# Two cross-attention layers on one core: layer 1's rows left unscaled before q, and a new order of the first batch's projections

## The chip, the cores and the metric

The kernel runs on one core of a Trainium2 chip. The core has a tensor engine (PE, with its weight loads shown apart as PEld), a vector engine (DVE), a scalar engine (ACT), a GpSimd engine (POOL) and a sync engine (SP), which here does nothing but issue DMAs. Each engine works through its own queue in order, and engines wait for one another on semaphores. The metric is the device time of one execution in microseconds (us); lower is better. All data is float32.

## The reference

The input x has the shape (4, 1024, 512) and a context of (4, 1024, 384) goes with it. Two cross-attention layers follow each other. Cut to what matters:

```
# layer 0: 16 heads of 64
h    = layernorm(x) * gamma + beta
Q, K, V = h @ Wq, ctx @ Wk, ctx @ Wv
attn = softmax(Q K^T) * 64**-0.5
x    = x + (attn V) @ Wo + bo

# layer 1: 16 heads of 32
xn   = x * rsqrt(mean(x*x) + 1e-5) * norm_w      # per row of x
q    = rotate((xn @ wq) by heads, cos, sin)
k, v = rotate((ctx @ wk) by heads, cos, sin), ctx @ wv
q    = q / max(norm(q), 1e-12)                   # per row and head
k    = k / max(norm(k), 1e-12)
out  = x + softmax(q k^T * sqrt(32)) v @ wout
```

In layer 1, q is brought to unit length per head. A factor that a whole row of x carries into q therefore drops out of q again, except in the comparison with 1e-12.

## The kernel before

**Batches.** The four batches run one after the other. In each, layer 0 goes through eight pairs of heads (p = 0 to 7) and, in each pair, eight blocks of 128 queries (`Attention0.step`). A step puts scores on PE (L366), takes the row maximum on DVE (L391), exponentials on ACT (L392), scales the rows on POOL (L397) and turns 32x32 blocks on DVE (L400); every second step sixteen DMAs on SP (L411, tile eT) finish the transposition, and a product with v (L427, tile av) follows two steps later. Layer 1 works in two halves of eight heads (`Attention1.step`): scores L576, exponentials L586, sums of the exponentials on DVE (L592 adds two tiles of 128x512, L596 two of 128x1024), products L615 and L626, and at the end of a block a reciprocal on DVE (L633).

**Filling work.** All other work for PE (projections, transposes, output products) is cut into units with a cost, kept in a queue (`Units`). Each attention step takes units from the queue until their costs fill the time that the step is given. The order of the units in the queue is written out by hand; units that cost 0.0 put nothing on PE. PE's instructions come out in the order in which units are taken.

**The rows of x.** `norm_units` makes, for each half of the rows of a batch (four tiles of 128 rows), the units "stats", "apply" and "turn". For layer 1, "stats" squares the rows on ACT with their sum as a second output (L222), and on POOL scales the sum and adds eps (L223, tile ve) and raises it to the power -0.5 (L168, tile rs). "apply" multiplies the four tiles by rs on DVE (L235, tile xn). "turn" transposes them on PE in four groups of four 128x128 blocks (L246, tile pth); each group fills one PSUM bank, which ACT copies out with the column factor norm_w (L252, tile hT). For layer 0 the same units do a layer norm (L216, L231, L248).

**The chains of q and k in layer 1.** `rotated_chains` projects two tiles of rows into one PSUM bank (L164, tiles q_p and k_p). `rotate` then squares it on ACT (L477), rotates it on DVE (L479 to L482; L479 to L481 read the bank, and the last of them frees it), sums the squares by heads (L484, tile q_s), and on POOL takes the maximum with 1e-24 (L486, tile q_m, 128x16), the power -0.5 (L168, tile q_r) and the product with the rows (L490, tile rot). Later the rows are transposed on PE (L498, tile q_t) and copied by ACT (L503). There are eight chains of q in a batch, four in each half of the heads. `weave` puts a chain's last part two chains behind its first.

**Between the layers.** The output products of layer 0's last two pairs go first (tile po, added to x by L294). Then come the statistics of the first half of the rows, a chain of k, the second last product of layer 0 (L427), "apply", "turn", and the first chain of q. The second half of the rows gets its statistics, "apply" and "turn" inside layer 1's first steps, between chains.

**PSUM.** `bank` hands out four banks in turn in layer 0 and three in layer 1 (the fourth then holds the attention product). A bank that comes round again can be written when its last reader is done.

**The start.** In the first batch nothing runs beside the loads, so the order is written apart (L676 to L684): "first" is done before the attention, "rest" is taken by its first three steps and must be used up when step 3 begins, "later" follows. The unit "begin" of pair p loads the weights of pair p + 1 (`pair_load`, L306, three DMAs on SP) into one of two buffers.

The functions that the change touches:

Of the kernel before, what the change touches and what calls it, by code (L numbers as in the profile page):

```python
# [28 lines left out]
F32 = mybir.dt.float32  # L32
AF = mybir.ActivationFunctionType
ALU = mybir.AluOpType
AX = mybir.AxisListType

P = 128
S = 1024
NT = S // P
DQ = 512  # L40
NQ = DQ // P
# [9 lines left out]
EPS = 1e-5  # L51
EPS_L2 = 1e-12
# [56 lines left out]
def xattn_kernel(ctx: ExitStack, tc: tile.TileContext, a: dict, out: bass.AP):  # L109
    nc = tc.nc  # L110
# [87 lines left out]
            for h in range(2)  # L198
        ]

    def norm_units(b, layer, hT, rows):

        got = {}

        def stats(h):
            src = got[h] = rows(h) if layer else got[h]
            rs = sb.tile([P, 4], F32, tag="rs", bufs=2, name=f"rs{layer}_{b}_{h}")
            ve = sb.tile([P, 4], F32, tag="ve", bufs=2, name=f"ve{layer}_{b}_{h}")
            mv = None
            if layer == 0:  # L210
                mv = sb.tile([P, 4, 2], F32, tag="mv", bufs=2, name=f"mv_{b}_{h}")
                for t in range(4):
                    st = sb.tile([P, 6], F32, tag="st", bufs=2, name=f"st_{b}_{h}_{t}")
                    nc.vector.bn_stats(st, src[t])
                    nc.vector.bn_aggr(mv[:, t, :], st)
                nc.gpsimd.tensor_scalar(ve, mv[:, :, 1], 1.0, EPS, ALU.mult, ALU.add)  # L216
                xn = src
            else:
                ss = sb.tile([P, 4], F32, tag="ms", bufs=2, name=f"ss_{b}_{h}")
                xn = [sb.tile([P, DQ], F32, tag="row", bufs=4, name=f"xn_{b}_{h}_{t}") for t in range(4)]  # L220
                for t in range(4):
                    nc.scalar.activation(xn[t], src[t], AF.Square, accum_out=ss[:, t : t + 1])  # L222
                nc.gpsimd.tensor_scalar(ve, ss, 1.0 / DQ, EPS, ALU.mult, ALU.add)  # L223
            rsqrt(rs, ve)
            got[h] = src, xn, mv, rs

        def apply(h):
            src, xn, mv, rs = got[h]
            for t in range(4):
                if layer == 0:  # L230
                    nc.vector.tensor_scalar(  # L231
                        xn[t], src[t], mv[:, t, 0:1], rs[:, t : t + 1], ALU.subtract, ALU.mult
                    )
                else:
                    nc.vector.tensor_scalar_mul(xn[t], src[t], rs[:, t : t + 1])  # L235
            got[h] = xn

        def load(h):
            got[h] = rows(h)

        def turn_over(h, k):
            if k == 0:
                hT.append(sb.tile([P, NQ, 512], F32, tag="hT", bufs=2, name=f"hT{layer}_{b}_{h}"))
            pp = bank(f"pth{layer}_{b}_{h}_{k}")
            for t in range(4):
                nc.tensor.transpose(pp[:, t * P : (t + 1) * P], got[h][t][:, k * P : (k + 1) * P], ident)  # L246
            if layer == 0:
                nc.scalar.activation(  # L248
                    hT[h][:, k, :], pp, AF.Identity, bias=cols[:, 1, k : k + 1], scale=cols[:, 0, k : k + 1]
                )  # L250
            else:
                nc.scalar.activation(hT[h][:, k, :], pp, AF.Copy, scale=cols[:, 2, k : k + 1])  # L252

        return [
            {
                "load": [(0.0, lambda h=h: load(h))],
                "stats": [(0.0, lambda h=h: stats(h))],
                "apply": [(0.0, lambda h=h: apply(h))],
                "turn": [(0.45, lambda h=h, k=k: turn_over(h, k)) for k in range(NQ)],
            }  # L260
            for h in range(2)
        ]
# [174 lines left out]
    TH = 2  # L437
# [10 lines left out]
        nc.sync.dma_start(wq, a["wq"][:, f0:f1].rearrange("(n p) m -> p n m", p=P))  # L448
        return wq

    def rotated_chains(dst, src, nk, w, name, tmp):

        hd, nh = HD1 // 2, TH * FH // HD1
        tiles = {}

        def heads(ap):
            return ap.rearrange("p (t h d) -> p t h d", t=TH, d=HD1)

        def spread(ap):
            return ap.unsqueeze(2).to_broadcast([P, TH, FH // HD1, ap.shape[2]])  # L460

        def project(t0, i, k):
            if i == 0 and k == 0:
                tiles[t0] = [bank(f"{name}_p{t0}")]
                if which["from"] == 0:
                    which["kept"] = which["n"]
            pp = tiles[t0][0]
            t = t0 + i
            lhsT = src[t // 4][:, k, (t % 4) * P : (t % 4 + 1) * P]
            matmul(pp[:, i * FH : (i + 1) * FH], lhsT, w(k), k == 0, k == nk - 1)  # L470
            if i == TH - 1 and k == nk - 1:
                rotate(t0, pp)

        def rotate(t0, pp):

            t1, t2, sq = tmp.take()
            nc.scalar.activation(sq, pp, AF.Square)  # L477
            c_, s_ = cos[:, t0 : t0 + TH, :], sin[:, t0 : t0 + TH, :]
            nc.vector.tensor_mul(heads(t1), heads(pp), spread(c_))  # L479
            nc.vector.tensor_mul(heads(t2)[:, :, :, :hd], heads(pp)[:, :, :, hd:], spread(s_[:, :, :hd]))  # L480
            nc.vector.tensor_mul(heads(t2)[:, :, :, hd:], heads(pp)[:, :, :, :hd], spread(s_[:, :, hd:]))  # L481
            nc.vector.tensor_add(t1, t1, t2)  # L482
            ss = sb.tile([P, nh], F32, tag="ss", bufs=2, name=f"{name}_s{t0}")
            nc.vector.tensor_reduce(ss, sq.rearrange("p (h d) -> p h d", d=HD1), AX.X, ALU.add)  # L484
            sm = sb.tile([P, nh], F32, tag="sm", bufs=2, name=f"{name}_m{t0}")
            nc.gpsimd.tensor_scalar_max(sm, ss, EPS_L2 * EPS_L2)  # L486
            ri = sb.tile([P, nh], F32, tag="ri", bufs=2, name=f"{name}_r{t0}")
            rsqrt(ri, sm)
            t1h = t1.rearrange("p (h d) -> p h d", d=HD1)
            nc.gpsimd.tensor_mul(t1h, t1h, ri.unsqueeze(2).to_broadcast([P, nh, HD1]))  # L490
            tiles[t0] = t1

        def turn_over(t0):
            t1 = tiles.pop(t0)
            pt = bank(f"{name}_t{t0}")
            for g in range(2):
                for i in range(TH):
                    nc.tensor.transpose(  # L498
                        pt[:, (g * TH + i) * P : (g * TH + i + 1) * P],
                        t1[:, i * FH + g * P : i * FH + (g + 1) * P],  # L500
                        ident,
                    )
            nc.scalar.copy(dst()[:, :, t0 * P : (t0 + TH) * P], pt.rearrange("p (g t) -> p g t", g=2))  # L503

        return [
            (
                [(0.44, lambda t0=t0, i=i, k=k: project(t0, i, k)) for i in range(TH) for k in range(nk)],
                [],
                [(0.45, lambda t0=t0: turn_over(t0))],
            )  # L510
            for t0 in range(0, NT, TH)
        ]
# [132 lines left out]
    def flat(lists):  # L645
        return [u for lst in lists for u in lst]

    def prepare_units(b):

        st = {"ct": [], "hT": [], "pairs": [{} for _ in range(NPAIR)]}  # L650
        w = {}
# [16 lines left out]
        def order(other):  # L668
# [7 lines left out]
            if b == 0:  # L676
# [2 lines left out]
                first = cts[0]["turn"] + norms[0]["stats"] + pairs[0]["k"][:NC_] + norms[0]["apply"]  # L679
                first += cts[1]["turn"] + pairs[0]["k"][NC_:] + norms[1]["stats"]  # L680
                first += norms[0]["turn"] + pairs[0]["q"][:NQ] + norms[1]["apply"]
                rest = pairs[0]["v"] + norms[1]["turn"] + pairs[0]["q"][NQ:]
                later = flat([pairs[1][c] for c in ("begin", "k", "q", "v")])
                return [(0.0, load)] + flat(loads) + first, rest, later  # L684
            return flat(
                [
# [28 lines left out]
    for b in range(B):  # L715
# [7 lines left out]
        for p in range(NPAIR):  # L723
# [30 lines left out]
            if p == NPAIR - 1:  # L754
# [2 lines left out]
                    xt, lambda n: pairs[n]["vals"], lambda n: wo[3][:, n % 2, :], f"po0_{b}_3", (6, 7)  # L757
                )
                xnT = []
                norms = norm_units(b, 1, xnT, lambda h: xt[4 * h : 4 * h + 4])  # L760
                v = []

                def begin_v():
# [44 lines left out]
        begin("q")  # L808
        kT, qT = kq["k"], kq["q"]
        kT1, qT1 = qk_tile(f"k1_{b}_1"), sb.tile([P, 2, S], F32, tag="raw", bufs=1, name=f"q1_{b}_1")  # L810
        q = rotated_chains(lambda kq=kq: kq["q"], xnT, NQ, lambda k, wq=wq: wq[0][:, k, :], f"q1_{b}_0", tmp)
        k1 = rotated_chains(lambda kT1=kT1: kT1, ct, NC_, lambda k, wk1=wk1: wk1[0][:, k, :], f"k1_{b}_1", tmp)
        q1 = rotated_chains(lambda qT1=qT1: qT1, xnT, NQ, lambda k: wq1[:, k, :], f"q1_{b}_1", tmp)

        work.add(flat(outs[:4]) + norms[0]["stats"] + k1[0][0] + [(AV, att.product)] + norms[0]["apply"])
        work.add(norms[0]["turn"] + q[0][0] + k1[1][0] + k1[0][2] + [(AV, att.product)] + flat(outs[4:]) + q[0][2])
        work.drain()

# [12 lines left out]
        for half in range(2):  # L831
            n = 0
            if half == 0:
                vs = value_chains(att1.v1, wv1, ct, f"pv1_{b}_1")
                first = [q[1], (norms[1]["stats"], [], []), vs[0], (norms[1]["apply"], [], k1[1][2]), k1[2]]
                rest = [(norms[1]["turn"] + q[2][0], [], q[2][2]), k1[3], q[3], q1[0], vs[1], q1[1], q1[2]]
                rest += [q1[3], vs[2], vs[3]]
                chains = first + rest
# [89 lines left out]
```

## Time and profile before

| what | value |
|---|---|
| median of 3 runs | 2922.01 us (2919.55 to 2923.83) |
| the profiled execution | 2913.88 us, its span 2912.1 us |
| PE busy | 2852.3 us (98%) |
| DVE busy | 2186.5 us (75%) |
| ACT busy | 1434.4 us (49%) |
| POOL busy | 935.1 us (32%) |
| L235, the product of rows with rs | 32 instructions on DVE, 13.4 us |
| L168 on rs, both layers | 16 instructions on POOL, 17.1 us |
| L486 on q | 32 instructions on POOL, 18.4 us |
| granted PE clock, mean | 0.999 |

The time of the profiled execution stands beside its span: the span goes from the first to the last instruction in the trace. A line of the trace's answers in order of time gives the start and the duration in us, the engine, the line of the kernel, the operation, the tile written and the tiles read, the shapes, how many instructions were merged, and in brackets how long the engine had stood idle before and for whom it had waited. A line of the waits gives who waited for whom, the sum in us, how often, and the longest. Where a matmul is counted, the trace shows two records for one float32 instruction.

### The profile page before, as it was taken

The page shows a single profiled execution, that of the slowest core. Times are in us where ns is not written, and L with a number is a line of the kernel's source. Part 1 is how long each engine was busy: PE and PEld are TensorE (multiplying, and loading weights), DVE is VectorE, ACT ScalarE, POOL GpSimd, SP SyncE. Part 2 cuts the span into 40 slices and gives each one's busy share as a digit, 9 for nine tenths or more (in the row PEclk, how much of TensorE's full clock was granted, in tenths as well). Part 3 has the DMA queues.
Part 4 walks back from the last instruction along what each step waited for, and adds up shares of the span by engine and source line. Part 5 has one row for each costly group of instructions (what it writes and reads, how often), then busy time and mean ns, then how long its engine had stood idle before and what let it go on. Part 6 is the DMA issues. An engine that isn't in the chain of part 4 may idle for free.

```text
span 2912.1 us, 66608 instructions
## 1 busy us (share of the span) xinstructions
PE 2852.3 (98%) x27336; PEld 1433.1 (49%) x27336; DVE 2186.5 (75%) x2952; ACT 1434.4 (49%) x2265; POOL 935.1 (32%) x776
## 2 busy tenths in 40 slices
PE   8999999999999999999999999999999999999998
PEld 4444455555444444555544445455554445445544
DVE  5677785878777778587777777858777777785877
ACT  4444444666534444466644444446664444444664
POOL 2343353420134335432024433534102343353300
PEclk9999999999999999999999999999999999999999
DMA  5887775010398777401039887730104988772000
GB/s 142 191 185 184 167 171 127 22 36 25 79 198 191 181 173 174 117 22 36 26 88 213 193 184 166 177 91 22 36 25 113 210 192 187 163 174 74 2 2 31
DMA packets 177553, 348.88 MB, mean 120 GB/s; under 512 B 37600, under 2 KB 93152, under 8 KB 177248
## 3 DMA queue, kind: packets, MB, share of 16 engines
q1 hardware_dynamic: 175920, 343.96, 50.1%
q8 instruction: 216, 3.54, 0.5%
q14 instruction: 89, 0.73, 0.1%
q10 hardware_dynamic: 1328, 0.66, 0.1%
HBM read 67.64 MB, written 8.39 MB: 26 GB/s over the span
## 4 chain that ended last, share of the span: by engine, by line
PE 84%; DVE 8%; SPq 3%; DMA 2%; issue 1%; ACT 1%; POOL 1%; DVEq 0%; ACTq 0%
PE s L366 16%; PE av L427 14%; PE po L164 11%; PE s L576 8%; PE pv L164 7%; PE pqT L164 7%; PE av L615 7%; PE pkT L164 5%; PE q_p L164 3%; SPq L411 2%; PE av L626 2%; PE k_p L164 2%; DVE both L592 2%; DMA eT<-e 1%; DVE both L596 1%
## 5 line engine op out<-in xcount | busy, mean ns | idle before, releaser
L391 DVE TENSOR_REDUCE m<-s 128x1 f32<-128x1024 f32 x512 | 603.0, 1219 | 374.9 <-PE s L366 374.4
L586 ACT ACTIVATE e<-s 128x1024 f32<-128x1024 f32 x512 | 496.7, 1022 | 312.4 <-PE s L576 303.9
L397 POOL TENSOR_SCALAR raw<-raw,li 128x1024 f32<-128x1024 f32 x256 | 286.1, 1118 | 724.2 <-DVE li L396 715.7
L366 PE MATMUL s<-qk 64*128 64x512 f32 x2048 | 515.5, 615 | 2.9 <-ACT e L392 2.2
L392 ACT ACTIVATE e<-s,m 128x1024 f32<-128x1024 f32 x256 | 282.9, 1110 | 466.5 <-DVE m L391 217.4
L392 ACT ACTIVATE raw<-s,m 128x1024 f32<-128x1024 f32 x256 | 285.3, 1115 | 454.8 <-DVE m L391 454.8
L427 PE MATMUL av<-eT,v 128*64 128x256 f32 x4096 | 470.1, 382 | 8.2 <-DMA eT<-e 6.9
L397 POOL TENSOR_SCALAR e<-e,li 128x1024 f32<-128x1024 f32 x256 | 286.0, 1118 | 474.3 <-DVE li L396 247.7
L592 DVE TENSOR_TENSOR both<-e 128x512 f32<-128x512 f32 x512 | 341.9, 700 | 114.2 <-ACT e L586 86.9
L427 PEld LDWEIGHTS av<-eT,v 128*64 128x64 f32 x4096 | 286.2, 137 | 227.2 <-issue 88.6
L366 PEld LDWEIGHTS s<-qk 64*128 64x128 f32 x2048 | 183.7, 186 | 281.5 <-issue 165.4
L576 PE MATMUL s<-q,k 32*128 32x256 f32 x4096 | 306.0, 401 | 5.8 <-ACT q L503 2.7
L400 DVE STREAM_TRANSPOSE e<-raw 128x1024 f32<-128x1024 f32 x256 | 309.9, 1228 | 0.4 <-DMA eT<-e 0.4
L400 DVE STREAM_TRANSPOSE e<-e 128x1024 f32<-128x1024 f32 x256 | 310.0, 1229 | 0.2
L576 PEld LDWEIGHTS s<-q,k 32*128 32x128 f32 x4096 | 192.1, 184 | 152.7 <-ACT e L586 71.4
L164 PE MATMUL pqT<-hT,w 128*64 128x512 f32 (+1 forms) x1216 | 240.6, 595 | 2.4 <-ACT hT L248 2.4
L164 PE MATMUL po<-wo,vals 128*64 128x512 f32 x1024 | 234.6, 596 | 0.0
L294 DVE TENSOR_TENSOR x<-x,po 128x512 f32<-128x512 f32 x200 | 131.2, 678 | 89.4 <-PE po L164 88.8
L164 PEld LDWEIGHTS pv<-w,cT 128*64 128x64 f32 (+1 forms) x3360 | 170.4, 132 | 41.6 <-issue 34.8
L164 PE MATMUL pv<-w,cT 128*64 128x128 f32 (+1 forms) x3360 | 184.3, 274 | 0.7 <-ACT hT L248 0.7
L164 PE MATMUL pkT<-cT,w 128*64 128x512 f32 (+1 forms) x912 | 183.7, 598 | 0.0
L596 DVE TENSOR_TENSOR both<-both 128x1024 f32<-128x1024 f32 x128 | 159.7, 1248 | 4.4
(81 smaller groups left out, 2784.6 us busy)
## 6 DMA issues: line engine op xcount, KB each, us to landing
eT<-e SPq DMA_DIRECT2D x2048, 128.0 KB, 2.4
xr<-in_x_dram SPq DMA_DIRECT2D x32, 256.0 KB, 3.8
wo<-in_Wo_dram SPq DMA_DIRECT2D x16, 512.0 KB, 4.7
x<-in_x_dram SPq DMA_DIRECT2D x32, 256.0 KB, 3.8
out_dram<-x SPq DMA_DIRECT2D x32, 256.0 KB, 2.6
w<-in_Wq_dram SPq DMA_DIRECT2D x31, 256.0 KB, 3.1
c<-in_ctx_dram SPq DMA_DIRECT2D x32, 192.0 KB, 3.8
wkv<-in_wkv_dram SPq DMA_DIRECT2D x16, 384.0 KB, 3.3
```

The costliest lines, as they stand in the source:

```text
L164: nc.tensor.matmul(o[rr], lhsT[:, rr], rhs, start=start, stop=stop)
L366: nc.tensor.matmul(sc[j][:, kb * 512 : (kb + 1) * 512], pr["qT"][r[j], i * P : (i + 1) * P], pr["kT"][r[j], kb * 512 : (kb + 1) * 512], st ...
L391: nc.vector.tensor_reduce(m[:, j : j + 1], sc[j], AX.X, ALU.max, negate=True)
L392: nc.scalar.activation(e[j], sc[j].rearrange("p (g s) -> p g s", g=4), AF.Exp, bias=m[:, j : j + 1], accum_out=l[:, j : j + 1])
L397: nc.gpsimd.tensor_scalar(e[j], e[j], li[:, j : j + 1], HD0**-0.5, ALU.mult, ALU.mult)
L400: self.turn = [lambda j=j: nc.vector.transpose(self.e[:, :, i % BQ * 2 + j, :], e[j]) for j in range(2)]
L427: nc.tensor.matmul(av[r[j], :W].rearrange("p (t a i) -> p t a i", t=BQ, a=4), pr["v"][:, k, r[j]], eT[:, j, :, :, k * 32 : (k + 1) * 32], ...
L576: nc.tensor.matmul(sc[j // 2][:, j % 2, c, :], kT[rr, g, k * P : (k + 1) * P], qT[rr, g, qb * WQ : (qb + 1) * WQ], start=True, stop=True,)
L586: nc.scalar.activation(e, sc[u], AF.Exp, scale=float(np.sqrt(np.float32(HD1))))
L592: nc.vector.tensor_add(self.both[:, kk, 2 * u : 2 * u + 2, :], es[u][:, :, 0, :], es[u][:, :, 1, :])
L596: nc.vector.tensor_add(self.both[:, 0], self.both[:, 0], self.both[:, kk])
L615: nc.tensor.matmul(self.av[rr, 0, :], v[g][:, 2 * kk + c, rr], es[j // 2][:, j % 2, c, :], start=first and c == 0, stop=end and c == 1,)
```

## The change

It has two parts. In layer 1 the rows of x are no longer multiplied by rs: "apply" is gone there, the power -0.5 of ve with it, and "turn" transposes x itself. Since q is brought to unit length, the factor matters only in the maximum with 1e-24, which was taken of the scaled q; the sum of squares of the unscaled q is compared with 1e-24 times (mean(x*x) + 1e-5) instead. That bound differs from row to row, so it lies in ve, and the maximum of a chain of q is two instructions of 128x8, one for each tile of rows, with a column of ve as operand, where it was one of 128x16 with a constant. The chains of k keep the constant. ACT's squares go into scratch tiles that nobody reads.

In the first batch the unit "begin" of pair 1 (the loads of pair 2's weights) and the keys of pair 1 go ahead of the second turn of x and the second half of pair 0's q, where they came after both.

```diff
@@ norm_units, stats, layer 1
-                xn = [sb.tile([P, DQ], F32, tag="row", bufs=4, name=f"xn_{b}_{h}_{t}") for t in range(4)]
                 for t in range(4):
-                    nc.scalar.activation(xn[t], src[t], AF.Square, accum_out=ss[:, t : t + 1])
-                nc.gpsimd.tensor_scalar(ve, ss, 1.0 / DQ, EPS, ALU.mult, ALU.add)
+                    square = sb.tile([P, DQ], F32, tag="row", bufs=4, name=f"sq_{b}_{h}_{t}")
+                    nc.scalar.activation(square, src[t], AF.Square, accum_out=ss[:, t : t + 1])
+                e2 = EPS_L2 * EPS_L2
+                nc.gpsimd.tensor_scalar(ve, ss, e2 / DQ, e2 * EPS, ALU.mult, ALU.add)
+                guard.append(ve)
+                return
             rsqrt(rs, ve)
@@ norm_units, apply
-                    nc.vector.tensor_scalar_mul(xn[t], src[t], rs[:, t : t + 1])
@@ rotated_chains, rotate
-            nc.gpsimd.tensor_scalar_max(sm, ss, EPS_L2 * EPS_L2)
+            if guard is None:
+                nc.gpsimd.tensor_scalar_max(sm, ss, EPS_L2 * EPS_L2)
+            else:
+                for t in range(TH):
+                    own = slice(t * nh // TH, (t + 1) * nh // TH)
+                    at = (t0 + t) % 4
+                    nc.gpsimd.tensor_scalar_max(sm[:, own], ss[:, own], guard[(t0 + t) // 4][:, at : at + 1])
@@ prepare_units, order, first batch
-                rest = pairs[0]["v"] + norms[1]["turn"] + pairs[0]["q"][NQ:]
-                later = flat([pairs[1][c] for c in ("begin", "k", "q", "v")])
+                rest = pairs[0]["v"] + pairs[1]["begin"] + pairs[1]["k"] + norms[1]["turn"] + pairs[0]["q"][NQ:]
+                later = pairs[1]["q"] + pairs[1]["v"]
@@ between the layers
-        work.add(flat(outs[:4]) + norms[0]["stats"] + k1[0][0] + [(AV, att.product)] + norms[0]["apply"])
+        work.add(flat(outs[:4]) + norms[0]["stats"] + k1[0][0] + [(AV, att.product)])
@@ layer 1, first half
-                first = [q[1], (norms[1]["stats"], [], []), vs[0], (norms[1]["apply"], [], k1[1][2]), k1[2]]
+                first = [q[1], (norms[1]["stats"], [], []), vs[0], ([], [], k1[1][2]), k1[2]]
```

More of the change, by code (lines that the diff above doesn't have):

```diff
@@ L199, in context_units, with norm_units @@
         ]
-    def norm_units(b, layer, hT, rows):
+    def norm_units(b, layer, hT, rows, guard=None):
         got = {}
@@ L206, in stats @@
             src = got[h] = rows(h) if layer else got[h]
-            rs = sb.tile([P, 4], F32, tag="rs", bufs=2, name=f"rs{layer}_{b}_{h}")
+            if layer == 0:
+                rs = sb.tile([P, 4], F32, tag="rs", bufs=2, name=f"rs{layer}_{b}_{h}")
             ve = sb.tile([P, 4], F32, tag="ve", bufs=2, name=f"ve{layer}_{b}_{h}")
@@ L229, in apply @@
             for t in range(4):
[L230 to L235, printed above, removed]
+                nc.vector.tensor_scalar(
+                    xn[t], src[t], mv[:, t, 0:1], rs[:, t : t + 1], ALU.subtract, ALU.mult
+                )
             got[h] = xn
@@ L449, in half_q_load, with rotated_chains @@
         return wq
-    def rotated_chains(dst, src, nk, w, name, tmp):
+    def rotated_chains(dst, src, nk, w, name, tmp, guard=None):
         hd, nh = HD1 // 2, TH * FH // HD1
@@ L759, in xattn_kernel @@
                 xnT = []
-                norms = norm_units(b, 1, xnT, lambda h: xt[4 * h : 4 * h + 4])
+                guard = []
+                norms = norm_units(b, 1, xnT, lambda h: xt[4 * h : 4 * h + 4], guard)
                 v = []
@@ L810, in xattn_kernel @@
         kT1, qT1 = qk_tile(f"k1_{b}_1"), sb.tile([P, 2, S], F32, tag="raw", bufs=1, name=f"q1_{b}_1")
-        q = rotated_chains(lambda kq=kq: kq["q"], xnT, NQ, lambda k, wq=wq: wq[0][:, k, :], f"q1_{b}_0", tmp)
+        q = rotated_chains(lambda kq=kq: kq["q"], xnT, NQ, lambda k, wq=wq: wq[0][:, k, :], f"q1_{b}_0", tmp, guard)
         k1 = rotated_chains(lambda kT1=kT1: kT1, ct, NC_, lambda k, wk1=wk1: wk1[0][:, k, :], f"k1_{b}_1", tmp)
-        q1 = rotated_chains(lambda qT1=qT1: qT1, xnT, NQ, lambda k: wq1[:, k, :], f"q1_{b}_1", tmp)
-        work.add(flat(outs[:4]) + norms[0]["stats"] + k1[0][0] + [(AV, att.product)] + norms[0]["apply"])
+        q1 = rotated_chains(lambda qT1=qT1: qT1, xnT, NQ, lambda k: wq1[:, k, :], f"q1_{b}_1", tmp, guard)
+        work.add(flat(outs[:4]) + norms[0]["stats"] + k1[0][0] + [(AV, att.product)])
         work.add(norms[0]["turn"] + q[0][0] + k1[1][0] + k1[0][2] + [(AV, att.product)] + flat(outs[4:]) + q[0][2])
```

## The prediction

> **What bounds the kernel now.** I read the page's busy times first, then who kept PE waiting, window by window, then the order of time around each place that the change touches.
>
> ```profile
> PE 2852.3 (98%) x27336; PEld 1433.1 (49%) x27336; DVE 2186.5 (75%) x2952; ACT 1434.4 (49%) x2265; POOL 935.1 (32%) x776
> ```
>
> PE is busy for 2852.3 of 2912.1 us at the full granted clock, so an instruction less on DVE, ACT or POOL is worth nothing in itself. Only a stretch in which PE stands still can shrink, and there are 60 us of those in all. PE's waits from 497 to 560 us, at the start of layer 1 in batch 0 (in us, times, longest), come back to the tenth in the other three batches:
>
> ```profile
> PE pth L246 <- DVE rot L481: 1.7, 1, 1.7
> PE av L626 <- DVE both L592: 1.6, 1, 1.6
> PE s L576 <- ACT q L503: 0.7, 1, 0.7
> PE q_t L498 <- POOL rot L490: 0.6, 1, 0.6
> ```
>
> The first and the last of them can be touched. Just ahead lies the first turn of x for layer 1, in order of time (start, us, engine, line):
>
> ```profile
> 475.19 1.67 DVE L235 TENSOR_SCALAR xn<-x,rs 128x512 f32<-128x512 f32 x4
> ...
> 475.43 0.37 ACT L136 COPY vals<-av 128x256 f32<-128x256 f32 x1 [2.86 <-PE av L427]
> 475.82 2.86 PE L246 MATMUL pth<-ident,xn 128*128 128x128 f32 x16 [0.44 <-DVE xn L235]
> ...
> 477.28 2.42 ACT L252 ACTIVATE hT<-pth,cols 128x512 f32<-128x512 f32 x4 [1.48 <-PE pth L246]
> ...
> 478.61 3.67 PE L164 MATMUL q_p<-wq,hT 128*64 128x256 f32 x32
> ```
>
> The sixteen transposes take 2.86 us here and 1.97 in the prologue: they are fed row tile by row tile by DVE, 0.40 us each. Then ACT copies four banks, 0.605 us each, and the projection of q starts when the second copy has freed its bank: 477.28 + 1.21 + 0.12 = 478.61.
>
> **Part 1, the first turn of each batch.** The eight products of a batch's two turns are DVE's, L235 (0.48 us each); the 32 of four batches take 13.4 us of DVE by the page's group, which count only through who waits. The rows of x are complete when the fourth L294 ends at 470.07, so without the products PE transposes as soon as the product before (L427) ends, at 475.38. The first bank is done at 475.38 + 3 x 0.123 + 0.273 = 476.02, and ACT, whose own copy of vals ends at 475.80, takes it 0.11 later: 476.13 instead of 477.28. Copies and projection follow at the same distances. What is late next is again ACT's second copy, so the whole chain moves by 1.15 us. From there to 497 us PE has no wait, so it keeps this. Four batches: -4.6 us. The exponent L168 (rs, 1.01 us) that goes too lay in idle time of POOL and had ended at 472.27, three us ahead of the products.
>
> **Part 2, the guard of q.** Each chain of q gets two maxima with a per-row bound, 128x8, for one of 128x16. Seven of the eight chains of a batch have several us between POOL's scaling of the rows and their transposes; their cover is the lag of two chains in the weave. The second chain has none: PE waits 0.57 us for it.
>
> ```profile
> 509.95 1.28 DVE L592 TENSOR_TENSOR both<-e 128x512 f32<-128x512 f32 x2
> 510.13 0.62 POOL L486 TENSOR_SCALAR q_m<-q_s 128x16 f32<-128x16 f32 x1 [15.66 <-DVE q_s L484]
> 510.83 3.20 POOL L168 TENSOR_TENSOR q_r<-q_m,nhalf 128x16 f32<-128x16 f32 x1
> ...
> 511.27 1.23 DVE L596 TENSOR_TENSOR both<-both 128x1024 f32<-128x1024 f32 x1
> ...
> 514.10 1.05 POOL L490 TENSOR_TENSOR rot<-rot,q_r 128x512 f32<-128x512 f32 x1
> ...
> 515.21 0.66 PE L498 MATMUL q_t<-ident,rot 128*128 128x128 f32 x4 [0.57 <-POOL rot L490]
> ```
>
> The same maximum takes 0.25 us with DVE elsewhere (485.72) and 0.62 here; the exponent 2.93 and 3.20. One reading fits both: a POOL instruction that starts while DVE adds two tiles of SBUF waits for that addition to end, less 0.13 us. The first addition ends at 510.60 (0.35 of wait, found 0.37), the second at 511.23 (0.27, found 0.27); a scaling that starts at 544.77 inside an L596 that ends at 545.62 takes 1.76 for 1.05 (0.72, found 0.71). Now one more instruction goes between. The first maximum ends at 510.70 as before; the second starts inside the second addition, is let in at its end and finishes at 511.32 (128x8 lies between the 0.19 of 128x4 and the 0.25 of 128x16: 0.22). The exponent starts 0.08 later, at 511.40, and L596 is running since 511.27. It waits till 512.50: 0.97 more, so it ends at 515.30, the scaling runs 515.38 to 516.43 instead of 514.10 to 515.15, and PE waits 1.28 us longer. Queued behind on POOL are only the guard itself and, ten us later, the next k_m. The lower bound is a second maximum alone: 0.22 + 0.08 less the 0.03 that the smaller first one saves, 0.27 us. I take 1.28, since the fit has three rows and misses none by over 0.02. Four batches: +5.1 us, between +1.1 and +5.1.
>
> [...]
>
> **Part 3, the second turn of each batch.** Here too the products go (516.55 to 518.23), after a wait of 2.85 us of DVE for rs. But the wait of PE is elsewhere:
>
> ```profile
> 523.17 0.60 ACT L477 ACTIVATE rot<-k_p 128x512 f32<-128x512 f32 x1
> ...
> 523.94 0.68 DVE L479 TENSOR_TENSOR rot<-k_p,cos 128x512 f32<-128x512 f32 x1
> ...
> 525.43 0.63 PE L246 MATMUL pth<-ident,xn 128*128 128x128 f32 x4 [1.67 <-DVE rot L481]
> ```
>
> The third bank of this turn is the one that k_p lies in, and DVE frees it with L481. DVE, relieved, could start L479 earlier, but L479 reads after ACT's square, which ends at 523.77 and stands behind two exponentials that PE's own scores release. L479 moves from 523.94 to 523.80: -0.14, four times -0.6 us. It would be -1.67 each if ACT's square were not in the way.
>
> **Part 4, the first batch.** Pair 1's keys (24 matmul records, 5.2 us) go ahead of the second turn, where PE waits 2.4 us:
>
> ```profile
> 36.04 1.11 ACT L392 ACTIVATE e<-s,m 128x1024 f32<-128x1024 f32 x1
> ...
> 37.14 2.78 ACT L248 ACTIVATE hT<-pth,cols 128x512 f32<-128x512 f32 x4
> ...
> 37.97 2.79 PE L164 MATMUL pqT<-hT,w 128*64 128x512 f32 x12 [2.45 <-ACT hT L248]
> ```
>
> ACT's copies hT wait behind the exponentials of the last scores, and moving the keys does not take the turn away from scores: the next block's scores come first, then four key records, then the turn. From those scores (37.9) to the end of the second exponential is 5.5 us as now; the copy of the second half of the keys (0.60) now stands there too and holds the bank of the turn's fourth group, 0.83 more to pqT: 6.94 us, in which PE has 1.92 (scores) + 0.87 (keys) + 1.97 (turn) = 4.76. It waits 2.2 us instead of 2.45: -0.25. Three DMAs move too: pair 2's weights (L306) are now issued ahead of the first 16 of eT on SP, and wait for the last reader of pair 0's, q's second half, at 48.5 us instead of 57.63. eT, ready at about 44.7, starts at 50.3 instead of 47.43, is issued by 60.4 at 0.63 us each and lands 2.4 us after its last issue at 59.8: 62.2. Its product stands at 63.00 now. Slack 0.5 us; at the longest landing of this row, 3.4, it costs 0.5. Part 4: -0.25, between -0.45 and +0.3.
>
> **The sum.** -4.6 + 5.1 - 0.6 - 0.25 = -0.35 us. The profiled execution lasted 2913.88 (span 2912.1 and 1.8 around it), 8.1 below the median of 2922.01; the difference is taken off the median: 2921.7.
>
> **The rivals.** First, no convoy on POOL: the second maximum costs 0.27, the sum is -4.6 + 1.1 - 0.6 - 0.25 = -4.35, 2917.7. For it: the margin at 511.27 against 511.40 is a tenth of a us. Against: DVE's queue is full there, so L596 follows at once. Second, slower: the delayed scaling now starts at 515.38 inside DVE's reciprocal L633, which in the changed order runs from 515.31 to 517.06. If a reciprocal holds POOL off like an addition, the scaling ends at 517.98 and PE waits 2.83 longer per batch: -4.6 + 11.3 - 0.6 - 0.25 = +5.9, 2927.9. It decides from the point at which the scaling starts after 515.31. Against it: a scaling at 552.27, with a reciprocal till 552.50, took 1.05, where an addition would have made it 1.15; only 0.1 us of evidence. Third, PE's wait at the third bank goes wholly with DVE's relief: 4 x 1.67 in place of 0.6 without the convoy, -10.4, 2911.6; against it stands ACT's square. Last, that the change removes no more than hidden work, so that part 1 fails: 5.1 - 0.6 - 0.25 = +4.25, 2926.3; against it stand the 0.44 us of idle and the 2.86 against 1.97.
>
> **How the numbers follow.** The forecast has 0.58, no convoy 0.21, the reciprocal 0.10, the third bank 0.06, nothing gained 0.05. A measurement of this kernel tells about 0.2%, 5.8 us, from no change. The forecast, no convoy and nothing gained lie inside it, but for 0.04 of no convoy with small extra gains; the reciprocal lies on its edge, 0.07 outside and 0.03 inside; the third bank outside; 0.01 more goes to each side. That gives 0.11 faster, 0.81 same, 0.08 slower. The range reaches from no convoy, less 1.7 for the spread of runs (the lowest is 2.5 below the median), to nothing gained (2926.3): 2916.0 to 2926.5. That leaves out 0.16, the reciprocal and the third bank; the upper bounds of the forecast itself, +0.55 from part 4, lie well inside.
>
> **What would show it.** Part 1: pth follows L427 without idle, takes about 2 us, q_p starts 2.1 us after L427's end in place of 3.2. Part 2: q_r of the second q chain takes about 3.9 us and PE's wait for POOL's scaling grows from 0.57 to about 1.85; at 0.85 the first rival holds, at 3.4 the second. Part 3: PE's wait for L481 stays near 1.5. Part 4: a wait for hT of about 2.2 before pqT, and none for eT at the first product. The forecast is wrong if the q_t wait stays below 1 us or the L481 wait goes.

## The result, and the profile after

The changed kernel took 2931.76 us (median of 6 runs, 2927.67 to 2936.67), the kernel before 2919.16 us beside it (2916.94 to 2923.83). The ratio is 1.0041, its 95% interval 1.0030 to 1.0053: slower by 12.6 us, where -0.35 had been forecast and 2926.5 was the upper end of the range. The profiled execution after lasted 2935.58 us, span 2933.8, mean granted clock 0.994 (before 0.999).

From the page, the busy times of the changed kernel:

```profile
PE 2858.7 (97%) x27336; PEld 1440.4 (49%) x27336; DVE 2173.3 (74%) x2920; ACT 1434.7 (49%) x2265; POOL 986.0 (34%) x800
```

DVE is 13.2 us less busy without its 32 products; POOL, which lost eight powers on rs, is 51 us busier all the same. PE stands still for 75 us instead of 60, and is itself 6.4 us busier with the same 27336 records: it ran slower somewhere. PE's waits from 497 to 560 us (us, times, longest):

```profile
PE q_t L510 <- POOL rot L502: 3.0, 1, 3.0
PE av L638 <- DVE both L604: 1.8, 1, 1.8
PE pth L252 <- DVE rot L487: 1.5, 1, 1.5
PE s L588 <- ACT q L515: 0.7, 1, 0.7
```

The wait for POOL's scaled rows has gone from 0.57 to 3.03 us, and it is 3.03 in each of the four batches. The wait for DVE's additions has grown a little too (1.56 to 1.82; its sister 65 us later 2.22 to 2.35). The second chain of q in order of time (L498, L170, L502, L604 and L608 were L486, L168, L490, L592 and L596 before):

```profile
509.74 1.28 DVE L604 TENSOR_TENSOR both<-e 128x512 f32<-128x512 f32 x2
509.92 3.06 POOL L498 TENSOR_SCALAR q_m<-q_s,ve 128x8 f32<-128x8 f32 x2 [15.28 <-DVE q_s L490]
511.05 1.23 DVE L608 TENSOR_TENSOR both<-both 128x1024 f32<-128x1024 f32 x1
512.20 1.29 DVE L604 TENSOR_TENSOR both<-e 128x512 f32<-128x512 f32 x2
513.06 3.22 POOL L170 TENSOR_TENSOR q_r<-q_m,nhalf 128x16 f32<-128x16 f32 x1
516.35 1.05 POOL L502 TENSOR_TENSOR rot<-rot,q_r 128x512 f32<-128x512 f32 x1
```

The two maxima alone take 3.06 us, against 0.61 for such a pair where DVE adds nothing (485.52). They end at 512.98, and the sum on record had them end 1.2 us after their start. By the fit of the prediction (a POOL instruction is let in when an addition ends, less 0.13 us) this pair was held up four times: the first maximum (1.20 us) by both additions of 509.74, the second (1.88 us) by L608 and by the first addition of 512.20.

The second new thing comes after that wait. Windows of the changed kernel (length, busy us of each engine and how many instructions, then the granted PE clock, the DMA share and GB/s):

```profile
500.00:510.00 10.00, 10.00 (x168) 5.96 (x172) 6.12 (x10) 7.35 (x15) 0.08 (x1) 1.00 0.01 2
510.00:520.00 10.00, 6.92 (x88) 3.40 (x84) 7.01 (x9) 5.02 (x8) 7.48 (x5) 0.92 0.01 2
520.00:530.00 10.00, 8.46 (x112) 4.99 (x112) 4.95 (x8) 5.73 (x8) 0.00 (x0) 0.91 0.01 2
```

The clock falls after the wait, and PE's next matmuls show it:

```profile
517.46 0.66 PE L510 MATMUL q_t<-ident,rot 128*128 128x128 f32 x4 [3.03 <-POOL rot L502]
518.04 1.66 PE L166 MATMUL k_p<-wkv,cT 128*32 128x256 f32 x16
519.63 2.09 PE L588 MATMUL s<-q,k 32*128 32x256 f32 x16
```

The same sixteen k_p took 1.07 us before and the same scores 1.15. From the start of q_t to the start of the second turn (L252, L246 before) it is 9.04 us here and was 7.46 before: one drop costs 1.6 us. Two narrower windows, the end of the wait and what follows it, show its length:

```profile
514.97:518.38 3.41, 0.93 (x12) 0.67 (x16) 2.68 (x3) 0.34 (x2) 2.60 (x3) 1.00 0.00 0
518.38:521.79 3.41, 3.41 (x36) 1.60 (x32) 0.00 (x0) 0.39 (x2) 0.00 (x0) 0.50 0.00 0
```

The granted clock is one half for 3.41 us, and full again after it. The first turn went as forecast:

```profile
476.37 2.09 PE L252 MATMUL pth<-ident,x 128*128 128x128 f32 x16
477.06 2.42 ACT L258 ACTIVATE hT<-pth,cols 128x512 f32<-128x512 f32 x4 [0.20 <-PE pth L252]
478.39 3.67 PE L166 MATMUL q_p<-wq,hT 128*64 128x256 f32 x32
```

No idle time ahead of pth, 2.09 us in place of 2.86, and the projection starts 2.0 us after it in place of 2.8.

### The profile page after: what moved, and what is told of

The parts are those of the page before. It is cut to its first block, busy times and chain, and to the rows that moved or that the text cites. A ratio compares the mean times of both kernels' runs of the same rounds, so it can differ in the third digit from the quotient of the medians.

```text
span 2933.8 us, 66593 instructions
## 1 busy us (share of the span) xinstructions
PE 2858.7 (97%) x27336; PEld 1440.4 (49%) x27336; DVE 2173.3 (74%) x2920; ACT 1434.7 (49%) x2265; POOL 986.0 (34%) x800
## 4 chain that ended last, share of the span: by engine, by line
PE 85%; DVE 6%; DMA 3%; SPq 2%; issue 2%; ACT 1%; POOL 1%; DVEq 0%; ACTq 0%
PE s L372 15%; PE av L433 14%; PE po L166 11%; PE s L588 8%; PE pv L166 8%; PE av L627 7%; PE pqT L166 7%; PE pkT L166 5%; PE q_p L166 3%; PE k_p L166 3%; PE av L638 2%; SPq L417 2%; DMA eT<-e 2%; DVE both L604 1%; DMA x<-in_x_dram 1%
## 5 line engine op out<-in xcount | busy, mean ns | idle before, releaser
L397 DVE TENSOR_REDUCE m<-s 128x1 f32<-128x1024 f32 x512 | 602.9, 1219 | 384.1 <-PE s L372 383.7
L433 PE MATMUL av<-eT,v 128*64 128x256 f32 x4096 | 471.8, 383 | 15.0 <-DMA eT<-e 11.2
L604 DVE TENSOR_TENSOR both<-e 128x512 f32<-128x512 f32 x512 | 343.3, 702 | 140.1 <-ACT e L598 110.3
L608 DVE TENSOR_TENSOR both<-both 128x1024 f32<-128x1024 f32 x128 | 156.8, 1225 | 4.4
```

Source lines behind the costliest of these rows:

```text
L397: nc.vector.tensor_reduce(m[:, j : j + 1], sc[j], AX.X, ALU.max, negate=True)
L433: nc.tensor.matmul(av[r[j], :W].rearrange("p (t a i) -> p t a i", t=BQ, a=4), pr["v"][:, k, r[j]], eT[:, j, :, :, k * 32 : (k + 1) * 32], ...
L604: nc.vector.tensor_add(self.both[:, kk, 2 * u : 2 * u + 2, :], es[u][:, :, 0, :], es[u][:, :, 1, :])
L608: nc.vector.tensor_add(self.both[:, 0], self.both[:, 0], self.both[:, kk])
```

## The experiments

Two theories stood at first. A: the two maxima with a per-row bound are held up twice each by DVE's additions; PE's wait of 3.03 us follows from that, and the fall of the clock follows from the wait. B: the new order of the first batch upsets the run. Others (C, D, F) were rivals on single points. All times are against the kernel before, run beside them on the same chip; 0.001 of the ratio is 2.9 us.

| kernel | ratio, 95% interval | q_t wait, each batch | L638 waits, each batch | drops after q_t waits | drops after L638 waits |
|---|---|---|---|---|---|
| before | | 0.57 | 1.56, 2.22 | 0 of 4 | 0 of 8 |
| changed (first time) | 1.0041 (1.0030 to 1.0053) | 3.03 | 1.82, 2.35 | 3 of 4 | 2 of 8 |
| e10, changed (again) | 1.0046 (1.0031 to 1.0060) | 3.03 | 1.82, 2.35 | 3 of 4 | 0 of 8 |
| e1, first batch's order alone | 0.9996 (0.9988 to 1.0005) | 0.57 | 1.56, 2.22 | 0 of 4 | 2 of 8 |
| e2, layer 1 alone | 1.0038 (1.0025 to 1.0052) | 3.03 | 1.82, 2.35 | 3 of 4 | 0 of 8 |
| e3, constant maximum 128x16 | 0.9980 (0.9969 to 0.9990) | 0.57 | 1.56, 2.22 | 0 of 4 | 1 of 8 |
| e4, maximum on DVE | 1.0040 (1.0024 to 1.0056) | 0.28 | 2.55, 2.83 | 0 of 4 | 7 of 8 |
| e5, two constant maxima 128x8 | 1.0004 (0.9992 to 1.0017) | 1.91 | 1.57, 2.22 | 1 of 4 | 0 of 8 |
| e6, one per-row maximum 128x16 | 0.9999 (0.9989 to 1.0010) | 1.91 | 1.57, 2.24 | 1 of 4 | 0 of 8 |
| e7, one addition of two tensors | 0.9988 (0.9979 to 0.9998) | 0.57 | 1.57, 2.24 | 0 of 4 | 2 of 8 |
| e8, changed, wait filled | 1.0014 (1.0003 to 1.0025) | 0.26, rest filled | 1.81, 2.34 | 0 of 4 | 2 of 8 |
| e9, addition, old first order | 0.9987 (0.9976 to 0.9998) | 0.57 | 1.57, 2.24 | 0 of 4 | 2 of 8 |

The waits come from one profile of each kernel, but are the same in its four batches to 0.02 us. A drop is counted where the 10-us slice with the end of the wait, or the next, has a granted clock below 0.995. L638 is the line L626 of before.

**e1: the first batch alone.** The kernel before with only this edit:

```diff
-                rest = pairs[0]["v"] + norms[1]["turn"] + pairs[0]["q"][NQ:]
-                later = flat([pairs[1][c] for c in ("begin", "k", "q", "v")])
+                rest = pairs[0]["v"] + pairs[1]["begin"] + pairs[1]["k"] + norms[1]["turn"] + pairs[0]["q"][NQ:]
+                later = pairs[1]["q"] + pairs[1]["v"]
```

> The kernel before with the new order of the first batch alone (pair 1's keys ahead of the turn of x); layer 1 is as before, with the products by 1/rms. Theory A (the loss lies in the guard of q): the profile of the changed kernel shows a new wait of 1.5 us for eT at the first product and about 1 us more by the end of batch 0's layer 0, so 1 us slower than before, between 0 and +2, with the q_t wait at 0.57 in every batch and the granted clock as before. Rival B (the new order upsets the weave of the first batch and costs most of the 12.6 us): +8 or more.

Measured: 2921.73 against 2922.71 us, the interval from -3.5 to +1.5 us. B is out. The two ends of the edit show in PE's waits of the first 120 us:

```profile
PE av L427 <- DMA eT<-e: 4.5, 2, 4.1
PE pth L246 <- ACT qk L136: 1.7, 1, 1.7
```

The wait of 2.45 us for ACT's copy hT is replaced by one of 1.75 us for ACT's copy of the keys, and eT is now late for its first product: 0.47 us here, 1.51, 1.16 and 1.04 in the profiles of the changed kernel, e3 and e10, and 0.43 to 1.14 in the five others that have the new order; the profiles of before, e2 and e9, with the old one, have no such wait. The long wait for eT at 107 us (4.1) comes with both orders and differs from profile to profile (1.2 to 4.1). Against each other nothing is left that this measurement can tell.

**e2: layer 1 alone.** The changed kernel with those two lines back.

> The changed kernel with the old order of the first batch: only the rows of x without 1/rms, and the guard of q with a per-row bound in two maxima. Theory A: all of the loss but the 1 us of the first batch, so +11.6 against before, between +9 and +13, PE's wait for the scaled rows of q's second chain at about 3.0 us in all four batches. Rival B (the order of the first batch): +4 or less.

Measured: 2933.90 us, +11.2 against before, q_t wait 3.03 in all four batches. Within the intervals, all of the loss lies in layer 1.

**e3: the old maximum in the changed kernel.**

```diff
-                for t in range(TH):
-                    ...
-                    nc.gpsimd.tensor_scalar_max(sm[:, own], ss[:, own], guard[(t0 + t) // 4][:, at : at + 1])
+                nc.gpsimd.tensor_scalar_max(sm, ss, EPS_L2 * EPS_L2)
```

> The changed kernel with the old maximum: one 128x16 against the constant, in place of two 128x8 against the row's bound; the bound itself is still formed. What is computed differs from the reference only where a row of q is next to nothing. Theory A (the two maxima with a per-row bound cost everything): the q_t wait falls back to 0.6, parts 1 and 3 (-4.6 and -0.6) and the first batch (+1) remain: about -4 against before, between -6 and -2, and the clock stays granted. Rival C (POOL is late at this place because the chain of x moved earlier and DVE's additions fall differently, whatever the maxima): the q_t wait stays above 2 us and the time within 3 us of the changed kernel's, +9 or more against before.

Measured: 2917.47 us, -5.2 (interval -9.1 to -2.9), q_t wait 0.57. What is left of the change is a gain of the size forecast for parts 1 and 3 (-4.6 and -0.6), and C is out.

**e4: the maximum on DVE.**

```diff
-                    nc.gpsimd.tensor_scalar_max(sm[:, own], ss[:, own], guard[(t0 + t) // 4][:, at : at + 1])
+                at = t0 % 4
+                bound = guard[t0 // 4][:, at : at + TH].unsqueeze(2).to_broadcast([P, TH, nh // TH])
+                halves = [v.rearrange("p (t h) -> p t h", t=TH) for v in (sm, ss)]
+                nc.vector.tensor_tensor(halves[0], halves[1], bound, ALU.max)
```

> The changed kernel with the maximum of the guard moved to DVE: one 128x16 against the two bounds of the row, spread over the heads, straight after DVE's sum of squares; POOL starts with the exponent. Everything of the reference is computed. Theory A: no maximum on POOL, one wait (the exponent behind the addition that runs), so the exponent starts near 510.1 and the scaling ends near 514.6 in batch 0; the q_t wait goes to 0.1 or less, -0.5 against before in each batch: -2 on top of -4, so -6 against before, between -8 and -3. DVE's 32 maxima of some 0.1 to 0.2 us each lie where DVE has room but push its additions by that much. Rival C (whatever the maxima, POOL is late here): the q_t wait stays above 2 us and the time near +10.

A miss: the q_t wait fell to 0.28, as theory A had it, and yet the time was 2933.04 us, +10.3. The reason is in the next column of the table: the waits for DVE's additions grew to 2.55 and 2.83. DVE and POOL hold each other off, and here it is DVE's turn. In order of time, this kernel's DVE and POOL ahead of the first of these waits:

```profile
545.95 1.28 DVE L604 TENSOR_TENSOR both<-e 128x512 f32<-128x512 f32 x2
546.98 1.16 POOL L502 TENSOR_TENSOR rot<-rot,q_r 128x512 f32<-128x512 f32 x1
547.27 1.95 DVE L608 TENSOR_TENSOR both<-both 128x1024 f32<-128x1024 f32 x1
```

L608 takes 1.23 us where POOL leaves it alone; here it starts while POOL's scaling runs and takes 0.72 more. Counted from the sum of squares, POOL's scaling starts 0.3 us earlier than in e3 and this addition 0.3 later, which puts the scaling ahead of the addition instead of behind it. By the waits this kernel should stand at -0.1 us: parts 1 and 3 with -5.3, the q_t wait with -1.2, the L638 waits with 4 x (0.99 + 0.61) = +6.4. The rest is about what the clock costs, which fell after 7 of these 8 waits (7 x 1.6 = 11 us): PE itself is busy for 2865.6 us here and for 2852.8 in e3, with the same number of records. No run took the clock out of this kernel.

**e5: two maxima, but constant.** In each of the two maxima, the constant in place of the column:

```diff
-                    nc.gpsimd.tensor_scalar_max(sm[:, own], ss[:, own], guard[(t0 + t) // 4][:, at : at + 1])
+                    nc.gpsimd.tensor_scalar_max(sm[:, own], ss[:, own], EPS_L2 * EPS_L2)
```

> The changed kernel with the two maxima 128x8 kept, but against the constant: no per-row operand. What is computed differs from the reference only where a row of q is next to nothing. Theory A (an instruction of POOL waits once for each SBUF operand that it reads beside DVE's additions; the maximum with a per-row bound reads two): each constant maximum waits once, behind the first and the second addition, the exponent then behind the third, so the two take about 1.2 us together and PE's q_t wait is about 1.85 in each batch, as the sum on record had it; time +1 against before from the waits (-4.6 + 5.1 - 0.5 + 1), up to +4 with the granted clock. Rival D (it is the number of instructions, and the kind of bound does not matter): the pair takes 3.0 us, the q_t wait 3.0 and the time +10.

Measured: 2924.46 against 2922.24 us; the interval is -2.3 to +5.0, and POOL in order of time:

```profile
507.67 1.20 POOL L497 TENSOR_SCALAR q_m<-q_s 128x8 f32<-128x8 f32 x2 [15.47 <-DVE q_s L490]
508.96 3.87 POOL L170 TENSOR_TENSOR q_r<-q_m,nhalf 128x16 f32<-128x16 f32 x1
512.91 1.13 POOL L501 TENSOR_TENSOR rot<-rot,q_r 128x512 f32<-128x512 f32 x1
```

This is the convoy that the prediction had drawn for the changed kernel, to a tenth of a us: the pair 1.20 us (1.19 had been drawn, 510.13 to 511.32), q_r 3.87 ("about 3.9"), the q_t wait 1.91 ("about 1.85").

**e6: one maximum with a per-row bound.**

```diff
-                for t in range(TH):
-                    ...
+                nc.gpsimd.tensor_scalar_max(sm, ss, guard[t0 // 4][:, t0 % 4 : t0 % 4 + 1])
```

> The changed kernel with one maximum 128x16 against one column of the bound: both row tiles of a chain get the bound of the first, which is the only thing that differs from the reference. Theory A (one wait for each SBUF operand): the one instruction waits behind two additions and takes about 1.2 us in the second chain of q, not 0.62, the exponent comes behind the third addition, PE's q_t wait is about 1.85. Rival D (the number of instructions alone): 0.62, the q_t wait back at 0.57, and the time as with the constant maximum, -5.

Measured: 2923.00 us, the interval -3.2 to +2.9, q_t wait 1.91. The group of all 32 (busy us, mean ns; then idle time ahead of it and who ended it):

```profile
L495 POOL TENSOR_SCALAR q_m<-q_s,ve 128x16 f32<-128x16 f32 x32 | 35.1, 1098 | 262.6 <-DVE q_s L490 262.6
```

The same group of e5, with twice as many instructions:

```profile
L497 POOL TENSOR_SCALAR q_m<-q_s 128x8 f32<-128x8 f32 x64 | 35.5, 570 | 261.8 <-DVE q_s L490 261.8
```

One maximum with a column costs as much as two with a constant. D is out: it is the per-row operand that adds a wait, not the number of instructions alone.

**e7: one addition of two tensors.** On POOL, q_s plus the bounds spread over the heads, the edit of e4 with `nc.gpsimd` and `ALU.add`.

> The changed kernel with the guard as one addition on POOL, 128x16 plus the two bounds of the row spread over the heads: q_s + bound in place of max(q_s, bound). The two differ only where a row of q is next to nothing. It reads two SBUF operands as the maximum with a per-row bound does, but as a two-tensor operation, like POOL's exponent and its scaling, which wait once in the profiles so far. Theory A1 (what waits twice is the form with a per-row bound): 0.6 us, q_t wait about 0.6, and about -5 against before, between -7 and -3. Theory A2 (any two operands wait twice): 1.2 us, q_t wait about 1.85, between 0 and +4.

Measured: 2919.15 against 2922.24 us (interval -6.1 to -0.6), and the group:

```profile
L498 POOL TENSOR_TENSOR q_m<-q_s,ve 128x16 f32<-128x16 f32 x32 | 17.4, 544 | 274.5 <-DVE q_s L490 274.5
```

It reads the same two tiles as e6 in half the time, so A1 holds: an operation of two tensors is held up once, the form with a column twice. It adds where e6 takes a maximum, but that a maximum is held up twice as such is ruled out by e5, whose maxima are held up once each. Why the column costs a wait of its own, no run shows: beside DVE's additions the maximum with a column takes 1.21 us and the addition 0.59, and the traces have nothing from inside an instruction.

**e8: the wait filled.** The changed kernel, with PE kept busy while it waits (pt is the bank that the transposes fill next):

```diff
+            if guard is not None and t0 == 2 and dst() is not None and name.endswith("_0"):
+                for _ in range(3):
+                    nc.tensor.matmul(pt, ident, bo, start=True, stop=True)
```

> The changed kernel with three matmuls 128x512 whose result is thrown away, put into the q_t bank ahead of the transposes of q's second chain: PE is busy in most of its wait of 3.0 us. The guard is as in the changed kernel. Theory E (the granted clock drops after a PE wait of about 3 us, at some 1.7 us a time, and that is the part of the loss that the waits themselves don't explain): the drops behind the q_t waits go, the time falls by 3 to 7 us against the changed kernel, to +5 to +9 against before. Rival F (the clock has no part in it, or drops elsewhere in their place): no change, +11 to +12, or more if the matmuls come into the way of the transposes.

Measured: 2927.07 against 2922.24 us, ratio 1.0014 (1.0003 to 1.0025); the changed kernel's two intervals begin at 1.0030. In order of time:

```profile
514.00 2.84 PE L510 MATMUL q_t<-bo,ident 128*128 128x512 f32 x6
517.10 0.66 PE L513 MATMUL q_t<-ident,rot 128*128 128x128 f32 x4 [0.26 <-POOL rot L502]
517.68 1.07 PE L166 MATMUL k_p<-wkv,cT 128*32 128x256 f32 x16
518.68 1.15 PE L591 MATMUL s<-q,k 32*128 32x256 f32 x16
```

POOL is as late as ever (its pair takes 3.06 us here too) and q_t starts as late behind it, but k_p and the scores run at full speed. Work that computes nothing makes the kernel 8 to 9 us faster than the same kernel without it, by the ratios (the two did not run beside each other); 3 to 7 had been expected. Three drops of 1.6 us are 4.8 of that; what lies above is no more than the width of the intervals. E holds, F is out.

**e9: the addition, with the old first order.** The edit of e7 with the two lines of e1 taken back.

> The guard as one addition on POOL, as in the run before (q_s + bound, which differs from the maximum only where a row of q is next to nothing), and the old order of the first batch. From the runs so far: the waits of layer 1 give -4.6 - 0.5 = -5.1 with PE's q_t wait at 0.57; the order of the first batch is worth between -1 and +1. So -5 against before, between -7 and -3; if the new order of the first batch is a gain, no better than the -3 of the addition with the new order.

Measured: 2916.73 against 2920.49 us, -3.8 (interval -7.0 to -0.6). With e7 at -3.1 the two orders of the first batch can't be told apart again. e3, e7 and e9 are the versions that beat both kernels; of these e7 and e9 keep a guard that goes with the row.

**e10: the changed kernel once more.**

> The changed kernel itself, beside the same runs of the kernel before, to put its interval beside those of the experiments: +12.6 was measured first; with the first-batch order worth about nothing it should stand where the rows of x alone stood, +11, between +9 and +14. Each of its profile's q_t waits 3.0 us, and the granted clock drops behind most of them, as the first profile showed in three batches of four.

Measured: 2935.01 against 2920.49 us, 1.0046 (1.0031 to 1.0060), the waits as before to 0.01 us, drops behind three of the four q_t waits.

## Why the prediction was wrong, step by step

**Part 1 was right.** pth follows the product without idle and takes 2.09 us. From where pth could first start to the first scores of layer 1 it was 21.81 us (475.38 to 497.19) and is 20.61 (476.37 to 496.98): -1.20 per batch, forecast -1.15. e3 shows it in the time.

**Part 2 failed, in one term: the price of the two maxima, each let in once (the first to end "as before", the second "0.22").** The convoy itself was read rightly: with constant bounds (e5) the pair, q_r and the q_t wait came out at 1.20, 3.87 and 1.91 us, and the time at +2.2 us with the forecast inside its interval. But the diff has a column of ve as operand. The trace of before had POOL instructions with a column in layer 0 alone (L397), none of them beside DVE's L592 or L596, and the prediction gave the maxima the price of constant ones of their size. With the column each is held up by two additions (e6: 1.21 for one): the pair takes 3.06 (1.20 and 1.88) instead of 1.2, and the q_t wait 3.03 instead of 1.85. That is +2.46 per batch, +9.8 in all where +5.1 stood; the upper bound "+5.1" of this step was no bound. e4 shows the other direction too: there DVE's L608 started second and took 1.95 us for 1.23. The size comes from e5 and e6.

**Two steps were left out.** First, POOL's later scaling also holds up DVE, and DVE's additions are what PE's L638 waits for: 1.56 to 1.82 and 2.22 to 2.35, +1.6 in four batches. For the first of them, the additions L604 start at 551.83 while the scaling runs (550.93 to 552.22) and take 2.77 us instead of 2.51; for the second, two additions at 611.37 beside the scaling (610.34 to 612.36) take 2.14 instead of 1.28. The trace of before had a row for this too: there one addition, L596 at 606.67, took 1.95 us for 1.23 beside the scaling L490 (606.17 to 607.53).

Second, the granted clock. In layer 1 a wait of 0.57 us was followed by a drop in 0 of 20 cases of the table, 1.91 in 2 of 8, 3.03 in 9 of 12; each drop costs about 1.6 us (one in the changed kernel's first profile, at 1969.04, lasted 6.83 us and cost 2.8). Three of four make +4.8, and e8 shows that this part goes when PE is kept busy. The profile of before had the row that could have warned: its last wait, 3.02 us, which ends at 2904.68, lies at the only lower clock of that profile (0.69 from 2900 to 2910 us, 0.50 from there to the end).

Which of these waits a drop follows can be read from the starts of the drops. In the changed kernel's profile the first three start at 518.38, 835.82 and 1245.42 us, the second and third 93 and 213 times 3.413 us after the first; in every profile with several drops they lie on such a grid. Cut into the stretches of this grid, the twelve profiles give, from 10 us on and at full clock, 51 stretches in which PE is idle for more than 2.0 us, and a drop follows every one; it follows none of those with less than 1.8 us, and 4 of 20 between. In the changed kernel's own profile the seven drops come after stretches with 1.93 us of idle (ahead of 1245.42) and with 2.13 to 2.49 us (the six others); from 10 us on, no other stretch at full clock has more than 1.87 us. The nine waits of 3.03 us with a drop had 1.93 us or more in one stretch; the three others were cut by its end, with 1.84 us at most on either side (1.29 and 1.73 in the changed kernel's fourth batch, at 2696.08). The two waits of 1.91 us with a drop lay whole in one stretch, the six others did not.

So whether a drop follows a wait depends on where the wait falls in the grid, and the stretch need not be idle throughout: more than 2.0 of its 3.41 us were always enough. Waits of 3.03 us were followed by a drop in 9 of 12 cases, and waits of 2.55 and 2.83 us in 7 of 8. Why the clock goes by such stretches, no run shows.

**Part 3 was right.** PE's wait for L487 is 1.54 us, forecast 1.53.

**Part 4 can't be told.** The wait for hT gave way to one of 1.75 us, a larger gain than the 0.25 forecast, but eT, given a slack of 0.5 us, was late by 0.43 to 1.51. e1 leaves -3.5 to +1.5 us.

**The sum with the measured terms:** -4.8 (part 1) + 9.8 (q_t) + 1.6 (L638) - 0.5 (part 3) + 4.8 (clock) = +10.9 us, beside +11.2 for e2 and +12.6 and +14.5 for the changed kernel. (The drops behind L638 are not in it: e1, with the waits of before, has two of them as well.)

**The rivals.** "No convoy" is refuted by e5. The slower rival had the sign and nearly the size of the q_t wait (3.4), but not the cause: DVE's reciprocal L645 ran from 515.29 to 517.03 and the scaling that started inside it, at 516.35, took its plain 1.05 us. "Nothing gained" is refuted by e3, and the third bank's wait did not go.

## What to carry to other kernels

An instruction that the trace of before doesn't show, here a POOL maximum with a per-row column, must not take the price of its nearest kin where another engine's instructions hold it up: bound it by one more wait than the kin has (1.21 us in e6, 0.62 with a constant), or bring the bound in as a second tensor (0.59 in e7). Before an idle engine's queue is lengthened by an instruction, look at the one place among its many where the waiting engine has no slack, and then at what the other engine's queue does in turn (e4). And once a wait of the matmul engine comes near 2 us, add to it the price of a clock drop, 1.6 us here, with the share of cases that the runs show (2 of 8 at 1.91 us, 9 of 12 at 3.03).

## What the runs showed of the hardware that was not expected

- POOL beside DVE's additions: a constant maximum 0.62 us (128x16, e3) or 0.61 (128x8, e5), a two-tensor addition 0.59 (e7), a maximum with a column 1.21 (e6); with DVE elsewhere 0.25, 0.24, 0.21 and 0.33. Only the last is held up twice.
- DVE beside POOL's scaling: an addition of 128x1024 that starts while the scaling runs took 1.95 us for 1.23 (e4, and in the trace of before at 606.67).
- The PE clock fell to one half for 3.41 us after 9 of 12 waits of 3.03 us, and 7 of 8 of 2.55 to 2.83: always when more than 2.0 us of idle lay in one stretch of a grid of 3.41 us, never below 1.8. With useless matmuls in the wait it fell after 0 of 4 (e8).
